# A pre-norm transformer block on one core: the first batch's gate and up products as seven block products, their weight sums made ahead of it, the down weights in eleven requests

## The chip, the core and the metric

The kernel runs on one core of a Trainium2 chip. A core has five engines that work side by side, each through a queue of its own: TensorE (PE) multiplies matrices, VectorE (DVE) and ScalarE (ACT) do elementwise work, GpSimd (POOL) does elementwise work in SBUF, and SyncE (SP) issues most of the DMA requests. PE writes its results to PSUM; everything else lies in SBUF, 128 partitions wide, or in DRAM. The engines wait for one another by semaphores. The metric is the device time of one execution in microseconds (us), lower is better.

## The reference

The input is 4 sequences of 512 rows of 512 floats. All is fp32.

```
x = x + attention(layernorm(x)) @ Wo     # 32 heads of 16, 8 key/value heads, rotary positions, causal softmax
y = x + (silu(h @ Wg.T) * (h @ Wu.T)) @ Wd.T      # h = layernorm(x), 1376 hidden features
```

For each batch the gate and the up product multiply a 512 x 512 matrix by a 512 x 1376 one. The change is to how this is done for the first of the four batches.

## The kernel before, in words

**Slots.** The attention of a batch is 8 groups of 4 heads. `slot(b, steps)` runs the 8 groups of batch b. A group has four visits (`visits`), each of them scores on PE (`both_scores`), the exponential on ACT, causal masks on POOL (`causal`, L1099) and row maxima on DVE (`all_greatest`), then a last visit and the averages (`averages`, L1121). Between the visits it calls `gap(n)`, which spends a share of the list `steps`, work of other stages, each step with an estimated cost in us; a step that costs 0 is taken along with its neighbour. So PE always has dense products between two visits. In the first slot (b = 0) the list holds the query, key and value projections of later batches (`rest1`, `rest2`, `rest3`, three such lists); in the second, the last of them, the output projection of batch 0 (`attended`, with the weights `wo_sb`), batch 0's gate and up layer, and half of its down product; in the third and fourth the same for batches 1 and 2; what is left for batch 3 runs at the end.

**The gate and up layer, two ways.** Batch 0 uses `ordinary(0)`: 10 blocks of 128 features, gate and up each a product over 4 blocks of 128 inputs, 512 rows at a time. Its weights come straight from the inputs (`load_f`, two requests of 256 KB), three blocks ahead in turn in the tile `shared`. Batches 1 to 3 use `seven(b, n, blocks)`, Winograd's form of Strassen's scheme on a 2 x 2 split: 10 units (5 pairs of blocks, gate and up in turn) of 256 features, each 7 products of 256 x 256 by 256 x 256 instead of 8. It needs sums of blocks on both sides. Those of the activations are four subtractions on DVE (`sums_of`, L682) into the tile `xnTs[1]`; those of the weights are made once: `copies(u)` copies three of unit u's blocks from the inputs to a DRAM tile `packed[u]`; `packs(u)` loads the four raw blocks, makes four sums of 128 x 256 on POOL (L640) and stores the sums to `packed[u]` (512 KB, L643). `load_blocks(kind, v)` then fetches the seven blocks of unit v in four requests: "a" (one block), "y", "v" and "w" (two each), to places in `flat`, which the projections' weights wq, wk, wv share until they are used up. Block sums of the products are made by DVE on the way out of PSUM, gates by ACT, DVE and POOL (L721). In all slots products are issued in strips of 32 output partitions (`narrow`, L299).

**Where the sums are made.** Before, in the second slot: `timed` puts loads, sums and stores of the 10 units at given times into the list, 8.2 us of steps apart, the load 9.9 ahead of its first sum; the raw blocks lie in `spare`, in `xnTs[1]`. There the output weights `wo_sb` are loaded once, at the start of the kernel. The down weights `wd_sb` share their tile with batch 3's queries, keys and values, which are stored to DRAM (`spilled`) in the second slot; after that one request of 2.5 MB and one of the remaining 96 rows (`load_down`) fetch the weights.

**POOL's side list.** `idle` is a list of POOL steps; `pool_steps(n)` in each gap takes n of them. Before, it is used in the third slot and later only, with n = 3, 2, 2, 0, 3 in the five gaps of a group.

**SP's queue.** The row maxima of a group are turned by DVE, stored to DRAM (`turned_round`, L1080) and loaded as rows into the queries of a later group (`laid_out`, L1089, L1091). These requests stand in the same SP queue as all weight loads and stores, in program order; a request that waits holds up those behind it.

## Time and profile before

Three runs: 846.48, 847.42 and 847.66 us, median 847.42. The profiled execution took 848.06 us, of which its span, from the first to the last instruction, is 845.8.

| stretch of the span, us | what runs | PE busy | DVE | ACT | POOL |
|---|---|---|---|---|---|
| 66 to 176 (110) | first slot from its second group | 104.1 | 81.5 | 58.3 | 67.2 |
| 176 to 357 (181) | second slot, batch 0's layer | 179.1 | 104.7 | 47.6 | 81.1 |
| 357 to 535 (178) | third slot, batch 1's layer in seven products | 176.3 | 125.1 | 50.5 | 74.6 |
| 535 to 707 (172) | fourth slot | 171.3 | 112.1 | 50.7 | 64.3 |

A line of the profile's timeline gives the start, the time, the engine, the line of the kernel, the operation, the tile written and those read, the shape, and how many instructions are merged; in brackets is the idle time ahead of it and what ended that. "L299" is line 299 of the kernel. A matmul of the program shows as two records. "SPq" is a request being issued, not the transfer. The granted clock of TensorE was 1.00 throughout.

### The profile page before, as it was taken

The page shows a single profiled execution, that of the slowest core. Times are in us where ns is not written, and L with a number is a line of the kernel's source. Part 1 is how long each engine was busy: PE and PEld are TensorE (multiplying, and loading weights), DVE is VectorE, ACT ScalarE, POOL GpSimd, SP SyncE. Part 2 cuts the span into 40 slices and gives each one's busy share as a digit, 9 for nine tenths or more (in the row PEclk, how much of TensorE's full clock was granted, in tenths as well). Part 3 has the DMA queues.
Part 4 walks back from the last instruction along what each step waited for, and adds up shares of the span by engine and source line. Part 5 has one row for each costly group of instructions (what it writes and reads, how often), then busy time and mean ns, then how long its engine had stood idle before and what let it go on. Part 6 is the DMA issues. An engine that isn't in the chain of part 4 may idle for free.

```text
span 845.8 us, 28256 instructions
## 1 busy us (share of the span) xinstructions
PE 822.5 (97%) x11980; PEld 452.2 (53%) x11980; DVE 545.5 (65%) x1601; ACT 231.3 (27%) x342; POOL 352.5 (42%) x514
## 2 busy tenths in 40 slices
PE   6999999999999999999999999999999999999998
PEld 5654444544333335333555555436655556788887
DVE  7877777778555554458677776686877633656632
ACT  1045654422232322222233232222323331011100
POOL 4575574773544344223265634532244444101130
PEclk9999999999999999999999999999999999999999
DMA  8533304003764742253344632325333534545811
GB/s 259 124 96 78 91 16 91 5 3 64 232 191 144 235 137 77 88 200 77 84 155 140 196 115 66 115 47 151 96 97 103 162 106 148 119 146 174 291 33 50
DMA packets 149517, 101.57 MB, mean 120 GB/s; under 512 B 59696, under 2 KB 137264, under 8 KB 149136
## 3 DMA queue, kind: packets, MB, share of 16 engines
q1 hardware_dynamic: 149104, 94.01, 38.3%
q10 hardware_dynamic: 288, 5.77, 1.8%
q8 instruction: 94, 1.54, 0.8%
q14 instruction: 31, 0.25, 0.1%
HBM read 78.32 MB, written 25.17 MB: 122 GB/s over the span
## 4 chain that ended last, share of the span: by engine, by line
PE 76%; DVE 12%; POOL 4%; DMA 3%; issue 2%; ACT 1%; SPq 1%; POOLq 0%; DVEq 0%; ACTq 0%
PE mm L299 38%; PE mm L296 14%; PE sc L993 12%; DVE junk L1039 6%; PE av L1121 6%; PE sc L1006 4%; PE mm L590 2%; POOL e L1099 1%; DMA shared<-packed 1%; PE mm L582 1%; DVE st L218 1%; DVE rot L358 1%; ACT e L1094 1%; POOL home L425 1%; POOL qa L978 1%
## 5 line engine op out<-in xcount | busy, mean ns | idle before, releaser
L1039 DVE CUSTOM_DVE_ANT_0 junk<-sc,mask 128x128 f32<-128x128 f32 (+3 forms) x512 | 251.2, 491 | 139.0 <-PE sc L1006 78.4
L1094 ACT ACTIVATE e<-sc 128x1024 f32<-128x1024 f32 (+1 forms) x192 | 165.5, 882 | 384.4 <-PE sc L1006 300.7
L299 PE MATMUL mm<-xnT,shared 128*32 128x256 f32 (+1 forms) x3520 | 244.2, 420 | 2.3 <-DMA shared<-in_wg 1.5
L1099 POOL TENSOR_SCALAR_AFFINE_SELECT e<-e 128x512 f32<-128x512 f32 (+2 forms) x192 | 105.7, 560 | 225.4 <-ACT e L1094 222.3
L299 PEld LDWEIGHTS mm<-xnT,shared 128*32 128x32 f32 x3520 | 116.9, 110 | 113.0 <-issue 62.8
L993 PE MATMUL sc<-home,qa 32*64 32x512 f32 (+6 forms) x2048 | 156.1, 421 | 6.5 <-DVE low L1039 3.0
L1006 PE MATMUL sc<-qa,home 32*64 32x512 f32 (+6 forms) x2048 | 152.2, 427 | 1.5 <-DVE low L1039 0.8
L993 PEld LDWEIGHTS sc<-home,qa 32*64 32x64 f32 x2048 | 66.8, 131 | 90.2 <-DVE low L1039 29.1
L1121 PE MATMUL av<-e,home 128*32 128x512 f32 (+3 forms) x1024 | 81.9, 438 | 1.8 <-POOL e L1099 1.6
L296 PE MATMUL mm<-xnT,shared 128*128 128x256 f32 x360 | 80.3, 383 | 1.0 <-DMA shared<-packed 1.0
L296 PEld LDWEIGHTS mm<-xnT,shared 128*128 128x128 f32 x360 | 68.3, 192 | 12.8 <-issue 2.2
L299 PE MATMUL mm<-wd_sb,home 128*32 128x256 f32 (+3 forms) x848 | 71.4, 470 | 0.0
L1006 PEld LDWEIGHTS sc<-qa,home 32*64 32x64 f32 x2048 | 58.8, 130 | 22.5 <-issue 8.7
L1121 PEld LDWEIGHTS av<-e,home 128*32 128x32 f32 x1024 | 30.5, 109 | 47.2 <-issue 35.0
L299 PEld LDWEIGHTS mm<-wd_sb,home 128*32 128x32 f32 (+1 forms) x848 | 28.2, 110 | 36.9 <-issue 28.2
L299 PE MATMUL mm<-wo_sb,cx 128*32 128x512 f32 x384 | 45.4, 595 | 0.0
L797 POOL TENSOR_TENSOR wd_sb<-home 128x256 f32<-128x256 f32 x15 | 11.4, 759 | 75.6 <-DVE home L721 75.3
L1039 DVE DVE_READ_ACCUMULATOR2_ANT low<- 128x1 f32 x512 | 42.4, 83 | 0.0
L221 POOL TENSOR_TENSOR rstd<-rstd,neghalf 128x1 f32<-128x1 f32 x24 | 16.0, 667 | 56.8 <-DVE rstd L220 56.7
L1145 POOL TENSOR_TENSOR inv<-us,inverse 128x256 f32<-128x256 f32 x32 | 20.9, 654 | 44.5 <-DVE inverse L1138 44.3
L359 POOL TENSOR_TENSOR rot<-rot,rope_sb 128x512 f32<-128x512 f32 x18 | 25.7, 1425 | 23.0 <-DVE rot L358 22.8
L721 POOL TENSOR_TENSOR home<-home,u 128x512 f32<-128x512 f32 x20 | 25.2, 1281 | 21.2 <-DVE u L757 21.2
(146 smaller groups left out, 855.6 us busy)
## 6 DMA issues: line engine op xcount, KB each, us to landing
shared<-packed SPq DMA_DIRECT2D x90, 256.0 KB
flip<-u SPq DMA_DIRECT2D x88, 64.0 KB
packed<-xnT SPq DMA_DIRECT2D x10, 512.0 KB
xnT<-flip SPq DMA_DIRECT2D x18, 256.0 KB
wd_sb<-differences SPq DMA_DIRECT2D x7, 640.0 KB
shared<-packed SPq DMA_DIRECT2D x30, 128.0 KB
rows<-in_x SPq DMA_DIRECT2D x14, 256.0 KB
out<-rows SPq DMA_DIRECT2D x13, 256.0 KB
```

Source lines behind the costliest of these rows:

```text
L296: nc.tensor.matmul(out, lhsT=lhsT, rhs=rhs, start=start, stop=stop)
L299: nc.tensor.matmul(out[c : c + 32], lhsT=lhsT[:, c : c + 32], rhs=rhs, start=start, stop=stop)
L359: put(lambda: engine.tensor_tensor(rot, rot, sin, ALU.mult))
L590: nc.tensor.matmul(ps[96:P, ts(q, P)], lhsT=rest_w[:, a, kq, 32 * q : 32 * q + 32], rhs=xnTs[0][:, kq, most:], start=kq == 0, stop=kq == N ...
L721: engine.tensor_tensor(g, g, t, ALU.mult)
L993: nc.tensor.matmul(dst[at : at + 64, :n], lhsT=qa[g][rows_of(r), q : q + 64], rhs=keys_of(g)[rows_of(r), :n], start=True, stop=True,)
L1006: nc.tensor.matmul(dst[at : at + 64, first_q:], lhsT=keys_of(g)[rows_of(r), k : k + 64], rhs=qa[g][rows_of(r), P * j + first_q :], start=True,
L1039: nc.vector.tensor_tensor_reduce(out=junk[:, :n], in0=src, in1=mask[:, T - n : T] if i else mask[:, T:], scale=-1.0, scalar=BIG, op0=ALU.a ...
L1094: nc.scalar.activation(dst, src, AF.Exp, scale=1.0 / math.sqrt(DH))
L1099: nc.gpsimd.affine_select(out=e[rows, heads, c : c + P], in_=e[rows, heads, c : c + P], compare_op=ALU.is_ge, fill=0.0, base=base, pattern ...
L1121: nc.tensor.matmul(av[32 * r : 32 * r + 32, P * j :], lhsT=v[:, j, 4 * (m // 2) + r, DH * (1 - hf) : DH * (3 - hf)], rhs=e[:, r, c : c + n ...
L1145: nc.gpsimd.tensor_tensor(us[m][:, :, hf, :], turned[0][:, :, hf, :], by, ALU.mult)
```

## The change

Batch 0's layer is made by `seven(0, 0, ())` in place of `ordinary(0)`. For this:

- The weight sums move ahead. Units 0 to 3 are packed in the first slot, by way of `idle`, one sum in each of the first two gaps of a group; their raw blocks lie in `wo_sb`. Units 4 to 9 are packed in the second slot, 1, 1, 1, 0 and 2 sums in its five gaps, with raw blocks in `homes[0]`, blocks 6 to 9, which the same layer later fills. Loads and stores are list entries of their own that are taken as soon as they are at the head: a unit's store after the second sum of the next one, the load of the unit after that behind the fourth sum.
- `wo_sb` is loaded at the end of the first slot (`load_out`), after all sums there have been issued and the last store.
- Two of the four activation sums of batch 0 lie in `rows[2]`, the others in `xnTs[1]` as for the other batches; two are made ahead of the layer, two after its first two products. The remainder of the features (`edge`) comes after the ten units.
- Blocks "a" and "y" of unit 0 are requested at the start of the second slot, "v" and "w" behind the last projection. All units from number 0 to 39 are counted through.
- The down weights are fetched in eleven requests of 256 KB (the last of 192), 4.5 us of steps apart.

```diff
-    spare = turn.rearrange("p (u f m) -> p u f m", u=2, f=4)
+    sums = [sums[:, n] for n in range(4)]
+    spares = (wo_sb.rearrange("p k t -> p (k t)"), homes[0][:, 6:10, :].rearrange("p f t -> p (f t)"))
+    spares = [t.rearrange("p (u f m) -> p u f m", u=2, f=4) for t in spares]
...
+    sums0 = [rows[2][:, n, :].rearrange("p (k t) -> p k t", k=2) for n in (0, 1)] + sums[2:]
...
     def pool_steps(n):
-        for _ in range(min(n, len(idle))):
-            idle.popleft()[1]()
+        while idle and (n > 0 or idle[0][0] == "load"):
+            tag, step = idle.popleft()
+            n -= tag != "load"
+            step()
...
-        t = spare[:, u % 2]
+        t = spares[u > 3][:, u % 2]
...
-        if v >= (B - 1) * whole:
+        if v >= B * whole:
...
-            v, a, f = (b - 1) * whole + u, u % 2, 2 * (u // 2)
+            v, a, f = b * whole + u, u % 2, 2 * (u // 2)
...
+        if b == 0:
+            return [*steps[:1], t[2], *steps[1:2], t[3], *steps[2:], *ends], t[:2]
...
     load_columns(wq_sb, wq, P, D)
-    load_w(wo_sb, wo)
...
-            pool_steps((3, 2, 2, 0, 3)[n])
+            pool_steps(((1, 1, 0, 0, 0), (1, 1, 1, 0, 2), *[(3, 2, 2, 0, 3)] * 2)[b][n])
...
-    def load_down():
-        whole = FF // P
-        load_w(wd_sb[:, :whole, :], wd[: whole * P, :])
-        nc.sync.dma_start(out=wd_sb[: FF - whole * P, whole, :], in_=wd[whole * P :, :])
+    def load_down(f):
+        rows_of_f = min(P, FF - f * P)
+        nc.sync.dma_start(out=wd_sb[:rows_of_f, f, :], in_=wd[f * P : f * P + rows_of_f, :])
...
-    slot(0, early)
+
+    def pack(us):
+        made = [packs(u) for u in us]
+        idle.extend(("load", load) for load, _, _ in made[:2])
+        for at, (_, combine, _) in enumerate(made):
+            for n in range(4):
+                idle.append(("sum", lambda n=n, combine=combine: combine(n)))
+                if at and n == 1:
+                    idle.append(("load", made[at - 1][2]))
+                if at and n == 3 and at + 1 < len(made):
+                    idle.append(("load", made[at + 1][0]))
+        idle.append(("load", made[-1][2]))
+
+    def load_out():
+        need("sum")
+        pool_steps(0)
+        load_w(wo_sb, wo)
+
+    early.insert(4, after(lambda: pack(range(4))))
+    slot(0, [*early, after(load_out)])
...
-    asides = []
-    for u in range(whole):
-        load, combine, store = packs(u)
-        at = 8.2 * u + 6.0
-        asides += [(max(at - 9.9, 0.5), load), (at + 5.0, store)]
-        asides += [(at + 1.0 * n, lambda n=n, combine=combine: combine(n)) for n in range(4)]
-    asides += [(6.0, spilled), (34.0, load_down), (34.1, load_rest)]
+    blocks = [after(lambda kind=kind: load_blocks(kind, 0)) for kind in "ayvw"]
+    layer, first_sums = seven(0, 0, ())
     start1 = [
         before[0],
+        *blocks[:2],
+        after(lambda: pack(range(4, whole))),
         *rest3[-24:-12],
         *before[1:],
-        after(lambda: load_f(0)),
-        *rest3[-12:-1],
+        *rest3[-12:-2],
         *behind,
+        rest3[-2],
+        first_sums[0],
         rest3[-1],
-        after(lambda: load_f(1)),
+        *blocks[2:],
+        first_sums[1],
     ]
-    blocks = [after(lambda kind=kind: load_blocks(kind, 0)) for kind in "ayvw"]
-    layer = [*ordinary(0), *edge(0), *tiles[:5], *blocks, *tiles[5:cut]]
-    slot(1, [*start1, *timed(layer, asides)])
+    asides = [(6.0, spilled), (34.0, load_rest)]
+    asides += [(20.0 + 4.5 * f, lambda f=f: load_down(f)) for f in range(NF)]
+    slot(1, [*start1, *timed([*layer, *tiles[:cut]], asides)])
```

More of the change, by code (lines that the diff above doesn't have):

```diff
@@ L675, in load_blocks, with sums_of @@
         nc.sync.dma_start(out=place(kind, v).rearrange("p f k m -> p f (k m)"), in_=src)
-    def sums_of(which):
+    def sums_of(which, b):
         x = xnTs[0]
         b11, b12, b21, b22 = (x[:, 2 * j : 2 * j + 2, 2 * P * h : 2 * P * h + 2 * P] for j in range(2) for h in range(2))
-        t1, t2, t3, t4 = (sums[:, n] for n in range(4))
+        t1, t2, t3, t4 = sums if b else sums0
         one, two, by = ((t1, b12, b11), (t2, b22, t1), (t3, b22, b12), (t4, b21, t2))[which]
@@ L687, in seven @@
         x, home = xnTs[0], homes[n]
-        rights = (x[:, 0:2, 0 : 2 * P], x[:, 2:4, 0 : 2 * P], x[:, 2:4, 2 * P :], *(sums[:, s] for s in (3, 0, 1, 2)))
+        rights = (x[:, 0:2, 0 : 2 * P], x[:, 2:4, 0 : 2 * P], x[:, 2:4, 2 * P :], *((sums if b else sums0)[s] for s in (3, 0, 1, 2)))
         once = rope_sb[:, 2 * NK * 96 : 2 * T]
@@ L764, in seven @@
             steps += unit(u)
-            if u % 2:
+            if u % 2 and b > 0:
                 steps.append(after(lambda p=u // 2: later_sums(b, n, p, (0, 1))))
-        t = [after(lambda s=s: sums_of(s)) for s in range(4)]
+        t = [after(lambda s=s: sums_of(s, b)) for s in range(4)]
         ends = edge(n)
+        if b == 0:
+            return [*steps[:1], t[2], *steps[1:2], t[3], *steps[2:], *ends], t[:2]
         steps[12:12] = [after(moved)]
```

## The prediction

> **What bounds the kernel now.** I read the page's busy shares first, then the windows cut at the slots, the waits of PE, and the timelines of PE, POOL and SP around the places that the change touches.
>
> ```profile
> PE 822.5 (97%) x11980; PEld 452.2 (53%) x11980; DVE 545.5 (65%) x1601; ACT 231.3 (27%) x342; POOL 352.5 (42%) x514
> ...
> PE 76%; DVE 12%; POOL 4%; DMA 3%; issue 2%; ACT 1%; SPq 1%; POOLq 0%; DVEq 0%; ACTq 0%
> ```
>
> ```profile
> 66.00:176.00 110.00, 104.12 (x2028) 51.06 (x2028) 81.47 (x286) 58.29 (x93) 67.17 (x98) 1.00 0.23 54
> 176.00:357.00 181.00, 179.08 (x2488) 69.45 (x2480) 104.68 (x342) 47.64 (x60) 81.06 (x120) 1.00 0.46 136
> 357.00:535.00 178.00, 176.32 (x3066) 89.22 (x3062) 125.13 (x370) 50.49 (x69) 74.57 (x108) 1.00 0.41 127
> ```
>
> The three windows (after the length: PE, PEld, DVE, ACT, POOL busy, clock) are the first, second and third slot; the layer of batch 0 runs in the second, that of batch 1, already in seven products, in the third. In the second PE idles 1.9 us of 181, at granted clock 1.00. So there TensorE work that goes is time that goes, and any wait that PE gains is time that comes. Of the 1.9, one wait has 1.46:
>
> ```profile
> 213.63 1.92 PE L299 MATMUL mm<-xnT,shared 128*32 128x512 f32 x16 [1.46 <-DMA shared<-in_wg]
> ```
>
> **The products.** Bursts of PE, one of ordinary products and two of block products:
>
> ```profile
> 252.25 3.64 PE L299 MATMUL mm<-xnT,shared 128*32 128x512 f32 x32
> ```
> ```profile
> 428.92 2.80 PE L299 MATMUL mm<-xnT,shared 128*32 128x256 f32 x48
> ...
> 432.59 3.66 PE L299 MATMUL mm<-xnT,shared 128*32 128x256 f32 x64
> ```
>
> Between x16 (1.92 us, the line before) and x32 a 512-wide record costs (3.64-1.92)/16 = 0.1075 us; a 256-wide one (3.66-2.80)/16 = 0.054. Removed: 20 halves x 4 k x 4 strips, each recorded twice, 640 x 0.1075 = 68.8 us. Added: 10 units x 7 products x 2 k x 4 strips x 2 = 1120 x 0.054 = 60.2. That is -8.6. By the groups' means (73.9 us for the 640; 170.3/2880 x 1120 = 66.2) it would be -7.7. I take -8.6, since both layers are cut into the same number of bursts by the attention, and keep -7.7 as the other end.
>
> **DVE, ACT, POOL in the second slot.** DVE loses 20 gating operations (10 x 0.687 + 10 x 0.688 = 13.8 us) and gains 10 x (0.683 + 0.691 + 0.425 + 0.688) = 24.9 us of block sums, 10 x 0.762 of gates and 4 operand sums (3.0): +21.7, so 126 us of some 178. The third slot has 125.1 of 178 and idles PE 1.7 us; from 422.8 to 513.6, where its ten units stand, PE waits 0.28 + 0.52 + 0.28 = 1.1 us. ACT gains ten copies at 0.364. POOL loses 40 weight sums at 0.731 and gains 24 of them and ten gates at 1.281: +1.1 us. Cost taken: the +1.1 of the third slot; bounds 0 and +3.5. The upper bound includes unit 6, whose first write into homes[0] must wait until the weight sums of unit 8, which now lie there, are stored; the store is issued ahead of that unit's first product, and DVE waits behind it for at most the 3.0 us that the store below takes.
>
> **The first slot.** POOL gains 14 weight sums in seven groups (two more at its end): 67.2 + 11.7 = 79 us of 110 if the two are counted. Two sums go ahead of or behind the first mask of each group. Pushing POOL's row of each group back by 0.73 at those places, its idle times of 0.3 to 4.3 us take it up in groups 1, 2, 4 and 5; in 3, 6 and 7 the masks of e1 come 0.4 to 0.5 later, those of e2 on time (0.63 to 0.68 idle ahead of them). Those of e2 release the key masking that PE awaits 0.17 us in most groups. Taken: +0.4; bounds 0 and +2 (all three pushes and their like reach PE). The loads for the first unit land under POOL's 3.71 us wait at 67 to 71.
>
> **wo comes late.** Its load stood at 12.8 us; PE needs it at 182.42. Now wo_sb holds weights until the last store of unit 3, and the load is put behind that store at the end of the slot. In POOL's order the last two sums stand behind the key rotation of that place and ahead of the key spreads:
>
> ```profile
> 175.10 0.62 POOL L1145 TENSOR_TENSOR inv<-us,inverse 128x256 f32<-128x256 f32 x1 [1.55 <-DVE inverse L1138]
> 175.76 1.80 POOL L359 TENSOR_TENSOR rot<-rot,rope_sb 128x512 f32<-128x512 f32 x1
> 177.64 1.28 POOL L363 TENSOR_TENSOR wd_sb<-wd_sb,rot 128x512 f32<-128x512 f32 x1
> 178.90 1.51 POOL L425 TENSOR_SCALAR wd_sb<-kr,rope_sb 128x512 f32<-128x512 f32 x2
> ```
> ```profile
> 182.42 3.64 PE L299 MATMUL mm<-wo_sb,cx 128*32 128x512 f32 x32
> ```
> ```profile
> 319.60 0.34 SPq L643 DMA_DIRECT2D packed<-xnT  x1
> 322.70 1.77 SPq L176 DMA_DIRECT2D xnT<-in_wu  x2
> ```
>
> The sums run from 178.9 to 178.9 + 2 x 0.78 = 180.5. The third fence is the same store of 512 KB and the load that waits until it has landed: 3.1 us from issue to issue. So wo's load is issued at 180.5 + 3.1 = 183.6, over a microsecond after PE wants it. Estimate of its landing: the large load of wd_sb began to move about 1.0 us after its issue (269.44, traffic from 270.5) and then ran near 400 GB/s, so 1.05 MB takes 2.6 us, and 0.3 for the release: 187.5. PE, whose later scores stand behind the output products in its queue, idles 187.5 - 182.4 = +5.1. Bounds: with no more than the 2.1 us of a small request (65.12 to 67.21, the 16 KB row store and the load that waits for it) +3.3; at the 250 GB/s or so of the copies of 512-byte rows (56 to 64 us) +6.7. The Trainium skill, "DMA: Bandwidth & Descriptors", section "Bandwidth", gives 6.15 us for 1 MB from HBM on the GpSimd path: by it the load would land at 189.8, the wait be 7.4 and the whole sum +1.8. It also asks for requests of 1 MiB or more, which speaks against this change's eleven of 256 KB.
>
> **The down weights.** One request of 2.5 MB (and a rest) becomes eleven, spread over the layer. SP spends 0.4 to 0.7 us on a request of this kind; the large one held the next loads up (3.56 us for one at 272.71), and PE did not idle for it. Cost 0: the cover is the layer itself, whose plan puts the last request 0.4 us of products ahead of the first down product, and 7 us ahead of the one that reads it. If that cover were gone, one 256 KB landing, about 2.5 us, would show. The 1 MB that is gone from the queue at 12.8 us: 0 too, as PE has no wait between 9.2 and 41.6.
>
> **Then POOL in the next group.** SP's queue has behind wo: the rows for the next group (5 requests, 2.7 us, not needed before the following group), two block loads, and the loads for unit 4. Unit 4's first load waits, by its semaphore, for wo itself: 187.5, the second 188.5, landing near 191.4 at the 1.05 us that 256 KB of 512-byte rows take. Unit 4's first sum stands in POOL's queue behind the first mask and waits there from 184 to 191.4. Behind it: two rotations (2.6), a sum (0.8), a power (0.6), the masks of e1 (1.9), a power that needs the second output tile, those of e2 (0.8): 191.4 + 0.8 + 2.6 + 0.8 + 0.6 + 1.9 + 0.6 + 0.8 = 199.5. PE, released at 187.5, reaches the averages over e2 near 198.1. So +1.4, less 0.22 there now: +1.2; bounds 0 and +3.
>
> **Start of the layer.** The 1.46 us wait goes, since blocks a and y come early. Late next: the second pair of products needs t2. Counted from the opening of the group's last score visit, PE needs 0.9 for it, 1.3 and 0.85 for projections, 1.1 for the transposes between them, 0.95 for the last visit, 2.2 for averages, 1.75 for two products: there at 9.05. DVE has the transposed tile at 4.05, then t1 (0.8), a rotation (1.35), four maxima (1.9), the turn (0.2), the read of av (0.65), a reciprocal (0.25) and t2 (0.7): 9.9. So +0.9, with DVE's next maxima behind it. And blocks v and w can only be loaded when wq_sb is free; they stand behind the row store (8.3 to 8.65) and unit 6's two loads (to 9.75), whose 512 KB move until 11.6; v lands at 12.6. PE is there at 9.9 + 0.9 + a visit of 0.9 = 11.7: +0.9. Net 0.9 + 0.9 - 1.5 = +0.3; bounds -1.5 and +2.5.
>
> **The sum** against the profiled run (848.06 us, of it 845.8 span; 0.64 over the median of 847.42): -8.6 + 5.1 + 1.2 + 0.3 + 1.1 + 0.4 = -0.5, so 847.6 for that run and 846.9 at the median.
>
> **The rivals.**
> 1. Faster: the wait for wo is mostly covered. For it: PE's chain to 182.4 has DVE waits of up to 0.5 in it, and the first slot could run late for PE and not for POOL; the wait's lower end is 3.3 and the next two terms can be 0. Then -8.6 + 3.3 + 0 + 0.3 + 1.1 + 0.4 = -3.5, 843.9; with no wait at all 840.6. Against it: store and load are in series, and both rows are there.
> 2. Slower: POOL is held by weight loads all through the slot. Each later unit's load is issued one or two gaps ahead of its first sum (unit 6's in the same gap), against 9.9 us of steps before. A load of two requests takes about 4.5 us from issue to landing (1.0 issuing, 0.9 start, 2.1 moving, 0.3 release), a gap with its score visit about 4. It decides once SP is held over 4 us ahead of a load, as it was 4.6 us once for a store, for then the masks of e1 or e2 come after PE's averages. Price: six units at 0.7 to 1 us, with the rest of the sum +4 to +5, 851 to 852. Against it: the masks stand a whole visit later, and in the third slot, with as many POOL steps, PE waited 0.28 us for masks.
> 3. The saving does not appear, as DVE becomes the bound in the second slot: 126 of 178 us would have to stall PE by more than the third slot's 125 did. Then +8 for the waits, 855. The third slot speaks against it.
>
> **How the numbers follow.** 0.2%, 1.7 us, is about what a measurement of this kernel can tell from no change. Forecast, within that: 0.37. Rival 1: 0.33. Rival 2: 0.27, rival 3: 0.03. The likeliest case's own range is 845.7 to 849.1. Range for all: the lower end lets wo's wait shrink to 0.3 with the rest as summed (-5.3, 842), the upper is rival 2's price (852); below and above lie about 0.1 each. Prediction 847.0.
>
> **What would show it.** In the timeline of PE a wait of some 5 us for wo_sb ahead of the first output products, near 182; POOL waiting for a load behind it; a wait for rows (t2) and one for blocks v where the layer opens; 1120 256-wide records more under xnT, shared and sums, at 0.054 us; no wait of PE over 0.6 us in the rest of the slot. Wrong it would be if wo lands before 184, or if masks show as PE's releaser group after group.

## The result, and the profile after

The changed kernel took 857.43 us (median of five runs, 851.09 to 858.29) against 847.32 us for the kernel before on the same chip. The ratio is 1.0109, with a 95% interval of 1.0077 to 1.0141: slower by 1.1%. The prediction was 847.0, between 842 and 852.

The profiled execution is the fastest of these, 851.09 us with a span of 849.1, 3.3 us over the span before. Its mean granted clock is 0.995. The other executions ran at 0.991 to 0.994, and have no trace.

The page of the changed kernel, busy shares and the chain by engine:

```profile
PE 816.3 (96%) x12460; PEld 469.7 (55%) x12460; DVE 567.4 (67%) x1635; ACT 233.7 (28%) x352; POOL 367.0 (43%) x524
...
PE 73%; DVE 13%; DMA 6%; issue 2%; POOL 2%; SPq 2%; ACT 1%; DVEq 0%; POOLq 0%; ACTq 0%
```

Its windows at the slots, cut as they were for before (after the length: PE, PEld, DVE, ACT, POOL busy, clock, DMA share, GB/s):

```profile
66.00:176.00 110.00, 104.32 (x2036) 51.11 (x2024) 82.77 (x286) 58.53 (x93) 78.28 (x112) 1.00 0.30 78
176.00:357.00 181.00, 168.12 (x2900) 84.50 (x2897) 122.33 (x364) 48.94 (x67) 82.68 (x112) 0.98 0.45 144
```

PE is busy 6 us less over the whole span, as was intended, and DMA has gone from 3% to 6% of the chain. In the second slot PE was idle 1.9 us of 181 before; now it is idle 12.9, and the clock is no longer 1.00. What PE waited for in that slot, in us in all, the number of waits and the longest (`shared<-packed` are weight blocks, `rows` of L687 is the activation sum t2 of the prediction, `e` are the masks):

```profile
PE mm L304 <- DMA wo_sb<-in_wo: 7.6, 1, 7.6
PE mm L304 <- DMA shared<-packed: 2.8, 2, 1.4
PE mm L304 <- DVE rows L687: 1.5, 1, 1.5
PE av L1128 <- POOL e L1106: 0.8, 2, 0.6
```

The wait for `wo_sb` in the timelines of SP (store, then load), PE and POOL:

```profile
180.02 0.32 SPq L648 DMA_DIRECT2D packed<-wo_sb  x1
184.60 0.39 SPq L178 DMA_DIRECT2D wo_sb<-in_wo  x1
```
```profile
189.78 5.16 PE L304 MATMUL mm<-wo_sb,cx 128*32 128x512 f32 x32 [7.60 <-DMA wo_sb<-in_wo]
```
```profile
193.97 0.73 POOL L645 TENSOR_TENSOR home<-home 128x256 f32<-128x256 f32 x1 [10.39 <-DMA home<-in_wg]
```

The store was issued at 180.0 and the load could only go out at 184.6. The burst that follows takes 5.16 us, where the same 32 records took 3.64 before: the clock had fallen. Windows of 1 us show it (the clock is the third number from the end):

```profile
185.00:186.00 1.00, 0.00 (x0) 0.00 (x0) 0.00 (x0) 0.00 (x0) 0.00 (x0) 1.00 0.24 72
...
187.00:188.00 1.00, 0.00 (x0) 0.00 (x0) 0.00 (x0) 0.00 (x0) 0.00 (x0) 0.50 1.04 408
...
191.00:192.00 1.00, 1.00 (x8) 0.22 (x4) 0.00 (x0) 0.00 (x0) 0.00 (x0) 0.50 0.79 200
...
193.00:194.00 1.00, 1.00 (x16) 0.38 (x12) 0.00 (x0) 0.00 (x0) 0.04 (x1) 1.00 1.14 309
```

PE fell idle at 182.2. At 186.1, 3.9 us later, the granted clock went to 0.50, and it came back at 192.9, 3.1 us after PE had started again. Those 3.1 us did half of that in work, so about 1.5 us were lost.

The span can be split at the reads of `av` that end each group (DVE's transposes `us<-av` in the timeline). The columns are the time to the first read, the first slot from its first to its seventh group, from there to the end of the second slot with PE's busy and idle time in it, the third slot, and the rest. The last six rows are experiments told below. The opening is no measure of the change: it took 65.3 to 67.8 us in these traces, and 67.7 in one of the kernel before that was altered in the second slot alone (the spill in parts, below).

| profiled execution, us | opening | first slot | to the end of the second: length | PE busy | PE idle | third slot | rest | span |
|---|---|---|---|---|---|---|---|---|
| before | 65.5 | 93.2 | 196.9 | 194.0 | 2.9 | 178.3 | 311.8 | 845.8 |
| after | 65.3 | 93.2 | 201.9 | 188.0 | 13.9 | 178.1 | 310.7 | 849.1 |
| wo early | 67.1 | 95.9 | 196.7 | 187.1 | 9.6 | 179.3 | 311.4 | 850.3 |
| wo early, no sums | 66.3 | 95.7 | 190.6 | 186.4 | 4.2 | 179.5 | 310.4 | 842.5 |
| wo early, start | 66.7 | 96.0 | 200.1 | 189.2 | 11.0 | 179.3 | 311.5 | 853.6 |
| wo early, once | 66.1 | 95.1 | 200.8 | 189.3 | 11.5 | 179.2 | 311.1 | 852.2 |
| start, spill in parts | 66.0 | 95.7 | 193.2 | 187.3 | 5.9 | 179.3 | 311.2 | 845.4 |
| three mended | 67.8 | 94.3 | 190.8 | 187.3 | 3.5 | 178.3 | 311.7 | 842.9 |

At full clock (the rows wo early, no sums, start with spill in parts, and three mended) the seven products are worth 6.7 to 7.6 us of PE's time in this stretch. The change lost more than that to idle time: 11 us in its profiled execution. The experiments ask where the idle time comes from.

### The profile page after: what moved, and what is told of

Read it like the earlier page. It is cut to its first block, busy times and chain, and to the rows that moved or that the text cites. A ratio compares the mean times of both kernels' runs of the same rounds, so it can differ in the third digit from the quotient of the medians.

```text
span 849.1 us, 29326 instructions
## 1 busy us (share of the span) xinstructions
PE 816.3 (96%) x12460; PEld 469.7 (55%) x12460; DVE 567.4 (67%) x1635; ACT 233.7 (28%) x352; POOL 367.0 (43%) x524
## 4 chain that ended last, share of the span: by engine, by line
PE 73%; DVE 13%; DMA 6%; issue 2%; POOL 2%; SPq 2%; ACT 1%; DVEq 0%; POOLq 0%; ACTq 0%
PE mm L304 35%; PE mm L301 15%; PE sc L1000 11%; DVE junk L1046 7%; PE av L1128 6%; PE sc L1013 4%; PE mm L595 2%; DMA shared<-packed 1%; DVE st L221 1%; PE mm L587 1%; DVE rot L363 1%; POOL e L1106 1%; DVE u L319 1%; DMA flip<-u 1%; DMA wo_sb<-in_wo 1%
## 5 line engine op out<-in xcount | busy, mean ns | idle before, releaser
L304 PE MATMUL mm<-xnT,shared 128*32 128x256 f32 x3680 | 220.0, 381 | 3.4 <-DMA shared<-packed 3.4
L304 PEld LDWEIGHTS mm<-xnT,shared 128*32 128x32 f32 x3680 | 123.5, 110 | 91.4 <-issue 30.0
L726 POOL TENSOR_TENSOR home<-home,u 128x512 f32<-128x512 f32 x30 | 37.8, 1282 | 27.8 <-DVE u L762 27.8
L722 ACT ACTIVATE u<-home 128x512 f32<-128x512 f32 x40 | 23.0, 623 | 62.0 <-DVE home L762 52.7
```

Of the source, the lines that this page charges most:

```text
L304: nc.tensor.matmul(out[c : c + 32], lhsT=lhsT[:, c : c + 32], rhs=rhs, start=start, stop=stop)
L722: nc.scalar.activation(t, g, AF.Tanh, scale=0.5)
L726: engine.tensor_tensor(g, g, t, ALU.mult)
```

## The experiments

The first theory was: (A) the late wo, with the half clock behind it, is a loss of its own, and the rest goes as forecast. Its rival: (B) POOL and the queues have no room for the new weight sums in the second slot, so that another wait takes its place. In the later experiments two mechanisms for B's waits are told apart: (C) bandwidth, as DMA is full in that stretch, and (D) order, as block loads stand behind other requests in SP's queue.

### The changed kernel once more

> The changed kernel, unaltered, to see a second profile of it. The profile at hand took 851.1 us, four further executions 857.3 to 858.3, at a mean granted clock of 0.991 to 0.994 against 0.995. Theory A (the wait for wo and the slow clock behind it): a typical execution waits longer for wo_sb than the 7.6 us seen, or stays at half clock for longer than the 6.75 us seen (186.0 to 192.75); its profile shows it between 180 and 205 us, and nothing elsewhere. Theory B (POOL and the loads through the second slot): the difference of 6 us lies behind 205 us, in waits for masks or blocks. Time 851 or 857 to 858 by both.

Measured: 856.14 us, ratio 1.0091 (1.0078 to 1.0105). The profiled execution took 853.8; PE's wait for wo was 8.02 us, the one for t2 1.48, those for packed blocks 1.74, 1.48 and, in the third slot, 1.34. The shape of the first trace repeats, with every wait a little longer.

### wo loaded at the start, the raw blocks elsewhere

```diff
-    spares = (wo_sb.rearrange("p k t -> p (k t)"), homes[0][:, 6:10, :]...
+    spares = (homes[3][:, 4:8, :].rearrange("p f t -> p (f t)"), homes[0][:, 6:10, :]...
...
     load_columns(wq_sb, wq, P, D)
+    load_w(wo_sb, wo)
...
         pool_steps(0)
-        load_w(wo_sb, wo)
```

> One part undone: wo_sb is loaded at the start, as before the change; the raw weight blocks of units 0 to 3 lie in blocks 4 to 7 of homes[3] instead, which stay free until batch 3's keys come. Theory A: no wait of PE for wo_sb, no fall of the granted clock near 186; the profile's 7.6 us of wait, 1.5 us of the slow clock and most of POOL's wait of 10.4 us go: 840 to 843 us, and all executions within 1 us of one another. Theory B: two or three us less than the changed kernel, 848 to 855, and executions still 6 us apart.

Measured: 852.15 us, ratio 1.0046 (1.0026 to 1.0067), where theory A had 840 to 843. PE no longer waits for wo, but another wait takes its place: the last store now reads `homes[3]` (it lies in the tile `wd_sb`, whose name the profile shows), which POOL's key spreads overwrite, and so POOL waits for it, and PE for POOL's masks. POOL, then PE:

```profile
186.18 0.77 POOL L430 TENSOR_SCALAR wd_sb<-kr,rope_sb 128x512 f32<-128x512 f32 x1 [4.08 <-DMA packed<-wd_sb]
```
```profile
195.97 1.93 PE L1128 MATMUL av<-e,home 128*32 128x384 f32 x16 [2.42 <-POOL e L1106]
...
228.78 1.07 PE L304 MATMUL mm<-xnT,shared 128*32 128x256 f32 x16 [2.90 <-DMA shared<-packed]
```
```profile
196.00:197.00 1.00, 1.00 (x8) 0.17 (x8) 0.00 (x0) 0.00 (x0) 0.93 (x2) 0.50 0.11 16
```

The window behind the first of these waits has the clock at 0.50; so has the stretch from 230.0 to 233.4 behind the second, where PE had been at work again for 1.2 us when the clock fell. A wait of 2.4 us was enough for it. This edit moved the wait rather than removing it, so it does not settle what wo alone costs.

### PE kept busy through the wait

```diff
+    def filled(step):
+        ps = bank()
+        for n in range(8):
+            product_of(ps, xnTs[1][:, n % NK, :P], xnTs[1][:, n % NK, :], True, True)
+        step()
+
+    first_out = before[1][1]
+    before[1] = (before[1][0], lambda: filled(first_out))
```

> The changed kernel with eight more 128x512 products over 128 inputs (64 records of 0.1075 us, 6.9 us in all) ahead of the first output product, made of xnTs[1] with itself and never read: work for PE where it would wait for wo_sb. Theory A with the clock as a cost of its own: PE's wait for wo_sb shrinks to about 1 us, the granted clock stays at 1.00 near 186 to 193, so the added work costs nothing and the slow clock's share goes: 849 to 850 us in every execution (the changed kernel: 851 or 857). If the clock plays no part (the wait alone is the cost): 851 to 858 as the changed kernel.

Measured: 857.83 us, ratio 1.0116 (1.0098 to 1.0133): no gain. The clock stayed at 1.00 from 180 to 229.5, and the first burst on wo takes 3.64 us again:

```profile
191.13 3.64 PE L304 MATMUL mm<-wo_sb,cx 128*32 128x512 f32 x32 [1.54 <-DMA wo_sb<-in_wo]
...
231.39 1.08 PE L304 MATMUL mm<-xnT,shared 128*32 128x256 f32 x8 [2.63 <-DMA shared<-packed]
```

So the half clock at this place does follow from the idle time. But here it is the small part of the loss, 1.5 us. The filler only covers the wait: wo comes when it comes (191.1 us here, 190.3 in the second execution of the changed kernel), and what follows is as late. The waits for blocks were longer here (2.63 us with the clock at 0.50 for 3.4 us behind it, and 2.62 us with the same near 486, in the third slot, which took 184.3 us in this trace against 178.9 in the second one of the changed kernel), and no gain is left.

### The late wo alone, in the kernel before

```diff
-    slot(0, early)
+    def late_wo():
+        for n in range(2):
+            part = wo_sb[:, n, : 2 * P]
+            nc.gpsimd.tensor_tensor(part, part, part, ALU.add)
+        nc.sync.dma_start(out=scrap, in_=wo_sb[:, :2, :]...)
+        load_w(wo_sb, wo)
+
+    slot(0, [*early, after(late_wo)])
```

> The kernel before the change with the late load alone: at the end of the first slot two POOL additions on wo_sb, a store of 512 KB from it to a scratch tile and a second load of wo_sb behind that store. Theory A: PE waits 5 to 8 us for wo_sb near 182, the clock falls to half some 4 us into the wait, as in the changed kernel: 847.4 + 6.5 to 9.5 = 854 to 857, perhaps more in executions that stay at half clock for longer. Theory B (wait absorbed or small on its own): under 851.

Measured: 856.26 us, ratio 1.0096 (1.0080 to 1.0111), so +8.3 us, as theory A had it. SP, then PE:

```profile
180.30 0.33 SPq L1323 DMA_DIRECT2D scrap<-wo_sb  x1
183.00 0.39 SPq L176 DMA_DIRECT2D wo_sb<-in_wo  x1
```
```profile
188.19 6.30 PE L299 MATMUL mm<-wo_sb,cx 128*32 128x512 f32 x32 [5.43 <-DMA wo_sb<-in_wo]
```

Two additions on POOL, a store and the load behind it cost the kernel before 5.4 us of waiting and then a burst of 6.30 us instead of 3.64, with the clock at 0.50 from 186.8 to 193.6. The store released the load after 2.7 us here, where it took 4.6 in the changed kernel. That alone is nearly the whole difference between the two kernels. It is not the whole explanation, as the next runs show, since the products' gain is missing as well.

### wo early

```diff
-  pool_steps(((1, 1, 0, 0, 0), (1, 1, 1, 0, 2), *[(3, 2, 2, 0, 3)] * 2)[b][n])
+  pool_steps(((1, 1, 1, 0, 0), (1, 1, 1, 0, 2), *[(3, 2, 2, 0, 3)] * 2)[b][n])
...
-    slot(0, [*early, after(load_out)])
+    early.insert(len(early) * 13 // 16, after(load_out))
+    slot(0, early)
```

> Three weight sums per group of the first slot in place of two, so that the last store of unit 3 and the load of wo behind it come in the seventh group and not at the slot's end; all else as in the changed kernel. Theory A (the wait of 7.6 to 8.0 us for wo, and the 1.3 to 1.5 us of half clock behind it, are a loss of their own): the wait is gone, no other takes its place above 1 us before 220 us, the first slot costs at most 1 us more, and the time is 847 to 848.5, level with the kernel before. Rival B (in the slot's first group PE is bound by POOL, which is held by unit 4's weight loads, so a wait for masks takes the place of the one for wo): 851 to 853, with a wait of 2 to 4 us for the masks between 186 and 200 us.

Measured: 851.11 us (ten runs, 847.34 to 856.4), ratio 1.0042 (1.0021 to 1.0064). The mechanism is A's: no wait for wo, none for masks above 0.6 us between 186 and 200. The time is B's. Two things take it up. The third weight sum per group costs the first slot 2.7 us, not the one expected (waits for masks, up to 1.53 us at 129). And the waits at the start of the layer have grown:

```profile
224.67 1.07 PE L304 MATMUL mm<-rows,shared 128*32 128x256 f32 x16 [1.77 <-DVE rows L687]
...
229.68 1.07 PE L304 MATMUL mm<-xnT,shared 128*32 128x256 f32 x16 [2.90 <-DMA shared<-packed]
...
303.91 1.93 PE L304 MATMUL mm<-xnT,shared 128*32 128x256 f32 x32 [1.69 <-DMA shared<-packed]
```

The clock stayed at 1.00 through this wait of 2.90 us, though it fell behind one of 2.42 us in the kernel with the raw blocks elsewhere.

### The same without the second slot's weight sums

```diff
-        after(lambda: pack(range(4, whole))),
...
-  src = packed[v % whole][:, blocks[0] ...
+  src = packed[v % whole % 4][:, blocks[0] ...
```

> As with wo early, but units 4 to 9 have no weight loads, no weight sums and no stores in the second slot; their products read the blocks of units 0 to 3 instead, so that PE, DVE and the block loads do the same work, and the output differs. What goes is 24 sums on POOL (18 us), twelve loads and six stores. Theory A (POOL and SP have room for them, apart from single waits for masks and blocks): 1 to 2 us below the kernel with wo early alone. Rival B (the second rival of the prediction: POOL held by weight loads in group after group): 4 to 6 us below it.

Measured: 844.07 us, ratio 0.9954 (0.9937 to 0.9971), 7.0 us below wo early, which is beyond even rival B's number. PE's waits from the seventh group to the end of the second slot:

```profile
PE mm L304 <- DVE rows L687: 1.5, 1, 1.5
PE av L1128 <- POOL e L1106: 1.1, 2, 0.9
PE sc L1000 <- DVE low L1046: 0.7, 2, 0.5
PE sc L1000 <- issue: 0.4, 1, 0.4
```

The waits for packed blocks, 4.6 us in that stretch with the sums, are gone, and those for masks are not. So the weight sums of units 4 to 9, with their loads and stores, cost some 5 to 7 us (5.4 less idle time in that stretch, 7.0 less in the median). By the waits, little of it comes from holding POOL (masks 1.6 and 1.1 us); most comes in the arrival of blocks. The sums and their transfers were taken out together, so this run alone does not part them. The executions of this kernel lie within 1.3 us of each other (843.39 to 844.63), against 9 us for the one with the sums.

### Order at the start of the layer

```diff
-        rest3[-2],
-        first_sums[0],
-        rest3[-1],
-        *blocks[2:],
-        first_sums[1],
+        together(rest3[-2], *first_sums),
+        together(rest3[-1], *blocks[2:]),
```

> As with wo early; and at the start of the layer both operand sums of the first layer stand directly behind the transposes on DVE, ahead of the maxima, and the requests for blocks v and w directly behind the last projection, ahead of the row store and the loads for unit 6. Theory A (those two orders alone make the wait of 1.47 us for t2 and the one of 1.4 to 2.9 us for the blocks near 230 us, with a half-clock stretch behind it in some executions): both are gone, and the time is 3 to 5 us below the kernel with wo early alone, 843 to 845. Rival B (PE waits for the same bytes a little later, since unit 6's loads and the stores now stand ahead of the blocks for the next products): within 1 us of the kernel with wo early alone.

Measured: 854.47 us, ratio 1.0073 (1.0052 to 1.0094), 3.4 us slower than wo early. Both waits named are gone (the one for t2 wholly, the block's is 0.32), and a longer one stands 14 us on. PE, then ACT's queue, then windows of 2 us:

```profile
243.79 3.64 PE L304 MATMUL mm<-xnT,shared 128*32 128x256 f32 x32 [5.63 <-DMA shared<-packed]
```
```profile
231.12 0.34 ACTq L1309 DMA_DIRECT2D spill<-wd_sb  x1
```
```profile
238.00:240.00 2.00, 0.16 (x4) 0.00 (x0) 1.27 (x7) 0.00 (x0) 1.85 (x4) 1.00 1.07 376
240.00:242.00 2.00, 0.00 (x0) 0.00 (x0) 0.00 (x0) 0.00 (x0) 2.00 (x2) 0.82 0.91 322
242.00:244.00 2.00, 0.21 (x4) 0.23 (x8) 0.00 (x0) 0.00 (x0) 0.03 (x1) 0.50 1.14 329
```

PE waits while DMA is full, at 320 to 380 GB/s. Two candidates: the spill (`homes[3]`, shown as `wd_sb`) of 2.8 MB in one request on ACT's queue, 7 us before the wait begins; or unit 7's loads, which held SP's queue from 233.65 to 236.3.

### Down weights in one request

```diff
-    asides += [(20.0 + 4.5 * f, lambda f=f: load_down(f)) for f in range(NF)]
+    asides += [(33.9, load_all_down)]
```

> As with wo early, but the down weights come in one request (and one for the last rows) at 33.9 us of the layer's plan, as in the kernel before. Prediction's step (eleven requests cost 0): within 1 us of the kernel with wo early alone. Rival (the requests, each 0.3 to 0.8 us of SP's time, stand ahead of block loads, and cause the waits of 1.2 to 1.5 us for packed blocks near 304 us): 1.5 to 3 us faster than that kernel, with no wait for packed blocks over 0.5 us between 270 and 330 us.

Measured: 858.69 us, ratio 1.0133 (1.0111 to 1.0156): 7.6 us slower than with eleven requests. Neither the prediction's step nor the rival foresaw that sign for one request. In the profiled execution (853.95) DVE and then PE stand behind a store:

```profile
291.19 0.69 DVE L743 TENSOR_TENSOR home<-mm,rope_sb 128x512 f32<-128x512 f32 x1 [7.41 <-DMA packed<-home]
```
```profile
293.16 1.93 PE L304 MATMUL mm<-xnT,shared 128*32 128x256 f32 x16 [3.54 <-DVE home L753]
```

This is the place that the prediction names for unit 6 (its first write into `homes[0]` waits for the store of unit 8's sums), with the store behind 2.5 MB of down weights.

### The spill in parts, with the new orders

```diff
-        nc.scalar.dma_start(out=spill, in_=homes[3])
+        pass
...
-    asides = [(6.0, spilled), (34.0, load_rest)]
+    def spilled_part(f):
+        nc.scalar.dma_start(out=spill[:, f, :], in_=homes[3][:, f, :])
+
+    asides = [(34.0, load_rest)]
+    asides += [(6.0 + 1.25 * f, lambda f=f: spilled_part(f)) for f in range(11)]
```

> The kernel with wo early and the two orders at the layer's start, and in it the spill of homes[3] (2.8 MB in one request on ACT's queue, 6.0 us into the layer's plan) becomes eleven requests of 256 KB, one each 1.25 us of the plan. Theory C (the wait of 5.6 us for a block at 243.8 in the kernel with the new orders is made by the spill: DMA is busy throughout while its 2.8 MB move, some 9 us, and the block's bytes stand among them): the wait falls below 1.5 us, and the time to 846 to 848 (854.5 less the 4 to 5 us and less 1.5 to 2 us of half clock). Rival D (the block is late because its request stands in SP's queue behind unit 7's loads, which wait for a store): the wait stays above 3 us, and the time at 852 to 855.

Measured: 847.36 us, ratio 0.9995 (0.9978 to 1.0012), 7.1 us below the same kernel with one request (6.6 by the ratios, as the two ran on different chips). The wait of 5.63 us is gone, the clock is at 1.00 throughout the slot, and PE's waits are down to these:

```profile
PE av L1128 <- POOL e L1106: 2.4, 3, 1.2
PE mm L304 <- DMA shared<-packed: 2.1, 3, 0.9
PE sc L1000 <- DVE low L1046: 0.7, 2, 0.5
```

Theory C, with its number.

### The units' loads and stores on POOL's queue

```diff
+        queue = nc.gpsimd if u > 3 else nc.sync
...
-        nc.sync.dma_start(out=packed[u][:, 3:, :], in_=t)
+        queue.dma_start(out=packed[u][:, 3:, :], in_=t)
```

(The two loads of a unit likewise.)

> The kernel with wo early (851.1), with the loads and stores of units 4 to 9 issued on POOL's queue and not on SP's; the same bytes move. Rival D (SP's queue, in order, holds the block loads behind these loads and stores): the waits for packed blocks near 230 and 304 us (2.9 and 1.7 us) fall below 1 us each, and the time towards that without sums, 845 to 848, unless issuing on POOL holds up the masks. Theory C (bandwidth: the bytes themselves, with the spill and the blocks, keep DMA full): the waits stay, 850 to 853.

Measured: 858.75 us, ratio 1.0123 (1.0108 to 1.0139), worse than either expectation. POOL itself now waits for its own store to land, which was issued at the moment when the spill set out (232.63 on ACT's queue):

```profile
232.33 0.57 POOL L650 DMA_DIRECT2D packed<-home  x1
...
245.12 1.53 POOL L637 DMA_DIRECT2D home<-in_wu  x2 [9.70 <-DMA packed<-home]
```
```profile
247.35 1.94 PE L1130 MATMUL av<-e,home 128*32 128x384 f32 x16 [4.19 <-POOL e L1108]
...
251.57 1.43 PE L1130 MATMUL av<-e,home 128*32 128x256 f32 x8 [2.27 <-POOL e L1108]
```

The store of 512 KB took over 12 us from issue to release, with DMA busy throughout, where the one ahead of wo's load took 4.6. The clock was at 0.50 from 246 to 256. One part of D is right, though: the wait of 2.90 us for blocks near 230 is gone here, and unit 6's loads are what has left SP's queue at that place.

> All of it together: wo early, the two orders at the layer's start, the spill in eleven requests, and units 4 to 9 on POOL's queue. If C and D each hold a part, no wait for t2 or for packed blocks above 1 us is left in the second slot, and the time is that without sums less the 1.5 us for t2 and plus 1 us for the masks: 843 to 845, faster than the kernel before. If POOL's issuing is dear (over 1 us each, eighteen of them), masks show as PE's releaser in every group and it is 848 or more.

With all edits together (these queues, the new orders, the spill in parts): 853.43 us, ratio 1.0064 (1.0041 to 1.0086). Not a wait for t2 or blocks is left in the second slot, but eight for masks, 6.7 us in all. A request on POOL's queue takes 0.6 to 0.9 us of POOL's own time, and the masks stand behind it. This is the case in which "POOL's issuing is dear".

### The spill in parts, alone, in both kernels

The same edit as above, in the changed kernel:

> The changed kernel, with nothing else altered than the spill of homes[3] in eleven requests (one each 1.25 us of the layer's plan). Theory C (the spill's one request is a loss of its own, whatever the orders at the layer's start): the wait for wo stays at 7 to 8 us with the clock at half behind it, the waits for blocks between 225 and 310 us sum to under 2.5 us, and the time is 850 to 852, so 5 to 7 us under the changed kernel. Rival E (the spill costs only where the blocks v and w are asked for early, as in the kernel with the new orders): 855 to 857, as the changed kernel.

and in the kernel before:

> The kernel before, with the spill in eleven requests. Theory C (in the kernel before PE waits for no block in that stretch, so the spill's bytes hold nobody up): 847 to 849, level with the kernel before. Rival F (the spill in parts is simply better, and is no part of the change's price): 843 to 845.

Measured: the changed kernel 855.02 us, ratio 1.0084 (1.0069 to 1.0099), so at most 1 to 2 us better than unaltered, which is nearer to rival E; the kernel before 848.23, ratio 1.0002 (0.9992 to 1.0013), unmoved. In the changed kernel PE stood 8.15 us for wo, and one of the waits at the layer's start was 2.59 us, with the clock at 1.00 behind it. So the spill is not what makes the changed kernel as it stands slow. I take it to matter once PE is no longer held up ahead of it, which is argued and not tested by itself. With the new orders it was issued at 231.1 while blocks were due; in the changed kernel it is issued at 237.7, with PE's idle time already behind it.

The trace of the kernel before with the spill in parts (849.39 us) also shows the half clock at a place that no edit here touches, from 44.6 to 48.0, with no long wait ahead of it:

```profile
44.42 4.51 PE L296 MATMUL mm<-wd_sb,shared 128*128 128x256 f32 x12 [0.60 <-DMA wd_sb<-flip]
```
```profile
46.00:47.00 1.00, 1.00 (x3) 0.74 (x3) 0.93 (x8) 0.74 (x3) 0.00 (x0) 0.50 0.03 11
```

PE was busy 77 to 82% of each of the three microseconds ahead of it. In the trace of the next experiment PE was as little busy there, and the clock stayed at 1.00.

### Three places mended

The changed kernel with wo early (three weight sums in each of the first four groups, two in the others), the orders at the start, the spill in parts, and the five requests that lay out the next group's rows put behind the first gap's block requests:

```diff
+            later_rows = g in range(10, 16) or g in range(18, 24)
+            if not later_rows:
                 laid_out(g + 1)
             for n, visit in enumerate(visits):
...
                 gap(n)
+                if n == 0 and later_rows:
+                    laid_out(g + 1)
```

> The changed kernel with wo early (three weight sums in each of the first four groups, two in the others, the load behind them in the seventh group), the two orders at the layer's start and the spill in eleven requests; further the five requests that lay out the next group's rows come, in the layers of batches 0 and 1, behind the block requests of the group's first gap and not ahead of them. If the waits of 0.9 us near 299 and 1.8 us near 476 come from these five requests ahead of the blocks in SP's queue, both fall below 0.3 us; the waits for masks near 129 us (1.25 us) go with the third sum of that group. Time: 843 to 845, faster than the kernel before. If the waits for blocks stay, bandwidth and not the queue's order makes them, and it is 846 to 847.

Measured: 845.76 us (twelve runs, 842.73 to 850.97), ratio 0.9974 (0.9956 to 0.9993): faster than the kernel before, though just above the 843 to 845 expected. PE's waits from the seventh group to the end of the second slot, and the window of that stretch in the kernel before and in this one:

```profile
PE mm L304 <- DMA shared<-packed: 1.3, 1, 1.3
PE av L1128 <- POOL e L1106: 1.0, 3, 0.6
PE sc L1000 <- DVE low L1046: 0.7, 2, 0.5
```
```profile
158.74:355.67 196.93, 194.04 (x2832) 77.78 (x2832) 117.19 (x386) 54.79 (x68) 91.80 (x132) 1.00 0.42 126
```
```profile
162.09:352.87 190.78, 187.25 (x3312) 94.36 (x3312) 136.99 (x421) 57.39 (x78) 94.85 (x126) 1.00 0.43 133
```

The wait near 299 is gone, the one near 476 fell from 1.81 to 0.80 us, not below the 0.3 expected, and the one for masks near 129 to 0.43. So the order of SP's queue made the first of these waits, and part of the second. One for a block at 229 has grown, from 0.81 to 1.32 us. Here the gain of the seven products arrives: 6.8 us less PE work in that stretch and 6.2 us less time. The first slot gives back 1.1 for its weight sums, and in the profiled execution the opening took 2.3 us longer than in the other trace, as it did in a trace of the kernel before (67.7 us).

## Why the prediction was wrong, point by point

**The products, -8.6 (other end -7.7).** Right in mechanism; 6.7 to 7.6 us at full clock, so just under the smaller end, that of the groups' means.

**wo comes late, +5.1 (3.3 to 6.7).** This is the step that failed first. The wait was 7.60 and 8.02 us, outside the bounds. The store's issue came as forecast (180.0 against 180.5). The term "3.1 us from issue to issue" was mis-sized, 4.6 us in this place (5.0 in the second execution), and the load took 5.2 us from issue to PE's first product against 3.9. Why the store held the load so long stays open: most of its bytes had moved by 182.4, after which the DMA share was 0.00 to 0.11 until the load's own bytes, and in the kernel before with the late wo a store of that size held the load for 2.7 us. By the figure of the Trainium skill's page "DMA: Bandwidth & Descriptors" (section "Bandwidth") the wait was put at 7.4, which came closer, by a different split.

**What is missing from the sum: the clock.** This is the step that failed in kind. "Any wait that PE gains is time that comes" left out what comes behind the wait. In the kernel before with the late wo the wait was 5.43 us, close to the 5.1 of the sum and inside its bounds, and the price was 8.3, since the burst behind it took 2.7 us longer. For waits up to 1.9 us the traces show no such addition. Behind the wait for wo the granted clock was 0.50, and the first 3 us of work counted half: +1.5 in the trace. The prediction put no price on the clock, which stood at 1.00 in the trace of before; it was the clock of a PE that was never idle for more than 1.46 us in that slot. The Trainium skill states the rule, in "TensorE: Matmul & The Clock Gate", Part 1: the clock gate goes to half after an idle window of about 3.4 us, a free-running one. The traces agree on the half, and their stretches at 0.50 are one, two or three times that long (3.4, 6.8 and 10.2 us). They differ on the idle time that it takes: the clock fell behind waits of 2.42, 2.62, 2.63 and 2.90 us too, and once with no wait over 0.60 us, so a wait shorter than 3.4 us is no safe bound here.

**wo's price as a whole.** In the kernel before, the late wo alone cost 8.3 us. Taking it out of the changed kernel gave 5.0 (856.14 to 851.11; 4 to 6 by the ratios, as the sets ran on different chips): the first slot then paid 2.7, and the waits behind it grew. I read the growth so: when PE is late, the blocks behind it have more time to arrive.

**POOL in the next group, +1.2.** POOL did wait as described, even longer (10.39 us, to 194.0 and not 191.4), and it cost PE nothing there. PE was later still, and slow.

**Start of the layer, +0.3.** The two new waits are those named, at the places named: t2 at 1.47 us against 0.9, the block at 1.44 against 0.9 (1.74 in the second execution). Net of the 1.46 that went this is +1.45 in the profile, inside the bounds of that step. The mechanism was right, the size was not.

**No wait over 0.6 us in the rest of the slot, +1.1.** Wrong: 1.41 us for a block at 304.6, behind the five requests that lay out the rows.

**First slot, +0.4.** Within its bounds: 93.2 us in both traces, so nothing.

**Down weights, 0.** Not contradicted: no wait of PE in the second slot is put down to them. What was not foreseen is that one request in their place costs 7.6 us, as measured in the kernel with wo early. The rule of requests of 1 MiB and more, which the prediction quoted from the Trainium skill's page "DMA: Bandwidth & Descriptors" (section "Bandwidth") as speaking against the change, concerns the bandwidth of the request itself. It gives no price for small requests that are due meanwhile, and here both requests of over 2 MB delayed such. The kernel before has both of them whole, and its PE waits for no packed block in that slot.

**The rivals.** Rival 2 (POOL held by weight loads, 851 to 852) named the right cost, the loads and stores of units 4 to 9, and a price not far off (7.0 us measured; six units at 0.7 to 1 us), but the wrong path. The sum itself held only +1.2 for POOL in the next group and +0.9 for blocks v behind unit 6's loads. Masks were PE's releaser for 0.8 us in the whole slot. The path is that of the blocks: `shared<-packed`, which the trace of before does not show as a wait in that slot. Its layer reads three blocks ahead straight from the inputs, where the seven products read one unit ahead; that this makes the difference is likely and was not tested. Rival 1 did not come about; rival 3 neither: with DVE busy 122 of 181 us, PE waited for DVE 1.5 us for t2 and, from the seventh group on, 0.7 for maxima.

**What stays open.** The prices that the experiments give come to about the measured loss: 6.7 to 7.6 us less for the products, 8.3 more for the late wo and 7.0 more for units 4 to 9 make +7.7 to +8.6, and the two sets measured +8.2 and +10.1. But prices that depend on one another (8.3 and 5.0 for the same wait) do not simply add. The profiled execution adds up (7.5 us less work, 1.5 lost to the clock, 11 us more idle time, 1.7 less elsewhere: +3.3 of span). The median execution was 6 us slower than it and has no trace. Its granted clock, 0.991 to 0.994, means 10 to 15 us at half clock (twice the missing share of the span) in place of the 8.5 that 0.995 gives (the trace shows 6.8 behind the wait for wo and about 1 at the span's end), so more or longer stretches of the kind shown. That they stand behind longer waits for blocks is likely, for two reasons: the kernels in which those waits are absent or short vary less (1.2 us without the sums, 3 us for the kernel before in its largest set); and among ten executions of wo early those at 0.999 or 1.00 took 847 to 852 us, the two at 0.996 took 855.0 and 856.4. But it is inferred. Even the mended kernel has executions of 850.0 and 851.0 us at 0.998 and 0.996, the one with the spill in parts has one of 851.1 at 1.00, and a trace of the kernel before shows a stretch at half clock behind no long wait.

## What to carry to other kernels

A wait on TensorE is priced as the wait and the half clock that may follow it once it reaches 2.4 us or so; two waits of 2.59 and 2.90 us came without it. Single waits up to 1.9 us cost no more than themselves in these traces, but one trace shows 3.4 us at half clock after several gaps of at most 0.6 us, so short gaps are not always free of it. Where weights are prepared just ahead of their use, add up the bytes that move in that stretch and look for the one large request in it: it can delay the small ones that are due, and cutting it up was worth about 7 us here, twice (once for the down weights, once for the spill). It depends on what else is due: the same cut of the spill gave nothing in the kernel before, and 1 to 2 us at most in the changed one. And take lateness apart in both directions: a delay put alone into the old kernel, and taken alone out of the new one, gave 8.3 and 5.0 us.

## What was not expected of the hardware

- The granted clock of TensorE fell to 0.50 between 2.0 and 4.7 us after PE fell idle, at times when PE had already started again. It stayed there for 3.4 us behind waits of 2.42 to 2.90 us, for 6.8 behind waits of 3.54 to 8.15, and for 10.2 behind waits of 4.19 and 2.27 in a row. A wait of 2.90 us brought it down in one kernel and not in another, and one of 2.59 did not. PE kept busy on other data through the wait did not lose it. In one trace it fell for 3.4 us where no wait had been over 0.60 us and PE 77 to 82% busy.
- A store of 512 KB from SBUF to DRAM released the load behind it after 2.7 us (the late wo in the kernel before), 3.1 (the kernel before, mid slot) and 4.6 to 5.1 us (the changed kernel and two variants), with little else moving; another released its reader over 12 us after its issue, beside a store of 2.8 MB on another engine's queue. What makes the difference is not known.
- A request issued by POOL took 0.6 to 0.9 us of POOL's time; the store and the load shown above took 0.3 and 0.4 us of SP's.
